# A transformer block on one core: another order for the preparation ahead of its main loop

## The chip, the cores and the metric

The kernel runs on one core of a Trainium2 chip. A core has a matrix engine (TensorE, PE in the profile, with PEld for its weight loads), VectorE (DVE), ScalarE (ACT), GpSimd (POOL) and SyncE (SP), each with an instruction queue of its own, and 16 DMA engines that all queues share. The metric is the device time of one execution in microseconds, as the median of several. The kernel before takes 727.65 us (three runs, 727.61 to 729.59).

## The reference, cut to what matters

One block for 16 samples of 256 tokens and 256 channels, 16 heads of 16 channels. Everything is float32.

```python
c_proj = silu(c) @ W_mod + b_mod          # c: 16 x 256, W_mod: 256 x 1536
shift_a, scale_a, gate_a, shift_m, scale_m, gate_m = split(c_proj, 6)
qkv = (ln(x) * (1 + scale_a) + shift_a) @ W_qkv + b_qkv      # q, k, v
x = x + gate_a * (softmax(q @ k.T * hd**-0.5) @ v @ W_proj + b_proj)
q_c = ln(x) @ W_qc + b_qc;  k_c, v_c = split(ln(context) @ W_kvc + b_kvc)
x = x + softmax(q_c @ k_c.T * hd**-0.5) @ v_c @ W_cproj + b_cproj
x = x + gate_m * (gelu((ln(x)*(1+scale_m)+shift_m) @ W_mlp1 + b_mlp1) @ W_mlp2 + b_mlp2)
```

## The kernel before, in words

Work is cut into 32 units: a self-attention ("s") and a cross-attention ("c") unit for each sample (`seq`, L824). Products that feed the softmax have to be more exact than one pass of the fast matmul type gives. So each operand is split into a high part (rounded to fp32r) and a low part (the rest), and a product is a sum of three: high by high, high by low, low by high (`mm3`, L463, goes through these three for the first half of the 256 input channels, then for the second).

For a unit, its normalised input `xn` is turned by TensorE into channel-major form (`psT`; word `T<n>t`), ScalarE scales it by 1 + scale_a while it rounds (`xTh`, word `T<n>h`), and VectorE makes the rest (`xTl`, word `T<n>l`). The products for keys and queries (`K<n>`, `Q<n>`) give `ps_k` and `ps_q`; ScalarE adds the bias and rounds (`h_k`, `h_q`), VectorE makes the rest (`l_k`, `l_q`), and three DMAs lay these rows into the "stack" `big[n % 3]` (`to_stack`, L523, `send`), in which the score matmuls find high and low parts on neighbouring partitions. A stack must have been zeroed (`z<n>q`, `z<n>k`: on POOL with the suffix p, on ScalarE with a) and have its rows of ones (`one<n>`).

The main loop (L1269) goes in beats, eight for each unit. In the beats of n = -1 only the scores of unit 0 are computed, and their maxima are reduced on VectorE (tile `mx`); the words of the table 'SL' are put between them. From n = 0 on, a beat holds the transposed scores and exponentials of unit n, the scores of unit n + 1, and the projections of later units.

The change touches what stands before that loop. `E_['PRE']` (L55) is a list of words. Each word calls a function that issues instructions on one or several engines (L1110); every engine's instructions, DMA issues on its queue too, keep the order of this list (`InOrder`, L40). So the list is the order of six queues at once, and a waiting instruction holds up all that follows it on its own engine. The words that matter here:

- `load` (L174): x of sample 0 on ScalarE's queue, on SP's queue W_mod for scale, the bias rows, W_qkv for keys, W_mod for shift, W_qkv for queries, x of sample 1, W_qkv for values. The condition `c_sb` is sent before it (L100).
- `silu` and `turn` (L185, L190): silu(c) is c * (tanh(c/2) + 1) / 2. Before: ScalarE's tanh and VectorE's product run on `c_sb`, 16 partitions by 256; then TensorE turns the result (`turn`) into 128 partitions by 32 and ScalarE halves it into `sT`.
- `b<n>` (L165): n matmuls of a tile of zeros into an unused bank; the profile shows each as two instructions.
- `brow`, `bp`, `bro2`: the bias rows, turned into columns.
- `scale`, `sc1`, `shift` (L218 to L224): columns of c_proj from `sT`, eight matmul instructions each, and VectorE's addition of the bias; `bk`, `bq`, `bv` (L227): the shift's share of the biases, from `shift` and the three parts of W_qkv.
- `hik`, `hiq`, `hiv` and `lok`, `loq`, `lov`: the split of W_qkv into `wself`.
- `L<n>a`, `b`, `d`: LayerNorm's statistics (VectorE), the power -1/2 (aggregation on VectorE, power on POOL), the application on VectorE.
- `lg`, `lc`, `lp`, `ld<n>`: loads for the gate, for the cross projection, for the projection, and of x of sample n.
- `K0a`, `K0m`: the key products of unit 0 for output channels 0 to 127 and 128 to 255; `K0h`, `K0l`: `h_k`, `l_k`; `K0x`, `K0w`, `K0yp`: the stack's transfers on SP, SP and POOL.

A DMA issue on SP can also be held by an older one: SP's issue of x of sample 2 stands idle until a part of W_mod has landed.

Of the kernel before, what the change touches and what calls it, by code (L numbers as in the profile page):

```python
# [10 lines left out]
F32 = mybir.dt.float32  # L11
F32R = mybir.dt.float32r
AF = mybir.ActivationFunctionType
ALU = mybir.AluOpType
AX = mybir.AxisListType

P = 128
# [4 lines left out]
def pixart_block(  # L22
# [8 lines left out]
    B, N, H = x.shape  # L31
# [4 lines left out]
    KC = H // P  # L36
# [15 lines left out]
                return tc.keep_in_program_order(i) if self.on else i  # L52
            return issue

    E_ = {'CUT': 8, 'LN': {'s': 'pool', 'c': 'pool', 'q': 'pool'}, 'ON': (1, 1, 1), 'L0': -16, 'L1': 1, 'S0': -7, 'A0': 0, 'T0': 1, 'S1': 5, 'A1': 7, 'L2': 9, 'T1': 9, 'S2': 32, 'AP': 99, 'DV': (0, 1), 'HP': (1, 0), 'BZ': {}, 'AV': {1: [(1, 2), (1, 3)], 9: [(0, 0), (0, 1)]}, 'AHEAD': (0, 0, 0, 0, 0, 2), 'TW': {(21, 6): 'cb', (23, 5): 'u0', (23, 7): 'u1', (25, 2): 'u2', (27, 3): 'u3', (27, 7): 'h2a', (28, 0): 'l2 h0p u5', (28, 2): 'h1p', (28, 4): 'h3p', (28, 7): 'u4 u6', (29, 0): 'l3d', (29, 1): 'l0', (29, 2): 'l1', (29, 7): 'h5p', (30, 1): 'u7 h6d h7p', (30, 3): 'h4p', (31, 1): 'l4 l6d', (31, 2): 'l5d x2', (31, 4): 'l7', (31, 7): 'b2'}, 'BE': 'G0 av P g0 A1 G1 G2 N1 F7 g1 S0 PF s2 p2 G3 a2 aT aL G4 x3 b3 S1 S2 T2 C r0 G5 S3 G6 S4 s3 CF x4 F8 g2 G7 S5 F9 p3 S6 G8 a3 r1 G9 F10 G10 T3 g3 b4 x5 x6 S7 s4 F11 S8 S9 F12 G11 p4 a4 F13 r2 S10 G12', 'XP': 1, 'IL': 1, 'MF': 0, 'SH': 4, 'RAMP': 1, 'HA': 1, 'MP': 16, 'W': (7, 1, 0, 0), 'PRE': 'load L0a z0kp z0qp L0b silu b15 hik turn L0d brow bp z1qa lok T0t lg scale b1 lc sc1 bro2 T0h T0l shift b3 ld2 one0 hiq loq L1a hiv K0a L1b bk K0m L1d bq K0h K0l Q0a L2a T1t T1h lp K0yp K0x z1kp Q0m T1l bv K1a Q0h K0w Q0x Q0yp Q0l lov K1b Q1a Q0w L2b Q1b K1l V0a K1y Q1l z2ka ld3', 'SL': {(-1, 0): 'V0b wm one1 L2c', (-1, 1): 'V1a T2t T2h', (-1, 2): 'K1wp T2p', (-1, 3): 'K1xp L3a Q1yp V1b ga', (-1, 4): 'M0 z2qa Q1xp Q1wp pb L3b vone gs', (-1, 5): 'mods0 ld4', (-1, 6): 'K2a K2m L3p', (-1, 7): 'L3c cb lx gm', (0, 0): 'sp3 mods1', (0, 1): 'sp0', (0, 3): 'sp1', (0, 4): 'sc2', (0, 6): 'one2', (1, 1): 'sp2', (1, 2): 'sp4'}}  # L55

    PE = InOrder(nc.tensor, True)
    ACT, DVE, POOL, SP = (InOrder(e, True) for e in (nc.scalar, nc.vector, nc.gpsimd, nc.sync))

    const = ctx.enter_context(tc.tile_pool(name="const", bufs=1))  # L60
    work = ctx.enter_context(tc.tile_pool(name="work", bufs=2))
# [3 lines left out]
    LONG, SHORT = "gen", "tr"  # L65
    ps_turn = [0]

    def ps_gen(name, tag=None):


        if tag is None and ps_turn[0] is not None:
            ps_turn[0] ^= 1
            tag = (SHORT, LONG)[ps_turn[0]]
        tag = tag or SHORT
        return psum.tile([P, 512], F32, tag=tag, name=name, bufs=2)
# [4 lines left out]
    ident = const.tile([P, P], F32, name="ident")  # L80
# [5 lines left out]
    big = [whole_big[:, 16 * N * i + 16:16 * N * (i + 1) + 16].rearrange("p (a k n) -> p a k n", a=2, k=8)  # L86
           for i in range(3)]
# [8 lines left out]

    BMOD, BQKV, BKVC, BM1 = 0, 12, 20, 24
    BQ, BK, BQC, BKC = 32, 34, 36, 38
    c_sb, th = [work.tile([B, 2, H], F32, tag=t, name=n, bufs=3)[:, 0] for t, n in (("qkh", "c_sb"), ("qkl", "th"))]
    SP.dma_start(c_sb, cond)  # L100
    X = {}

# [7 lines left out]
    brow = const.tile([32, P], F32, name="brow")  # L110
# [26 lines left out]
    sc1 = const.tile([P, 2, 2, B], F32, name="sc1")  # L137
    bT = const.tile([P, 40], F32, name="bT")
    sT = const.tile([P, KC, B], F32, name="sT")
    cb = const.tile([P, H], F32, name="cb")  # L140
# [43 lines left out]

    def f_silu():  # L185
        ACT.activation(dummy, mhalf, AF.Tanh)
        ACT.activation(th, c_sb, AF.Tanh, scale=0.5)
        DVE.scalar_tensor_tensor(th, th, 1.0, c_sb, ALU.add, ALU.mult)

    def f_turn():  # L190
        pst = st[:, 1, 480:]
        for k in range(KC):
            PE.transpose(pst[:, k * B:(k + 1) * B], th[:, k * P:(k + 1) * P], ident[:B, :B])
        ACT.mul(sT.rearrange("p k b -> p (k b)"), pst[:, :KC * B], 0.5)

    odd_rows = []

# [100 lines left out]
    wm = []  # L298
# [9 lines left out]
    gm = []  # L308
# [154 lines left out]
    def mm3(dst, W, f, xT):  # L463

        n = 0
        for k in range(KC):
            for a, b in ((W[0], xT[0]), (W[0], xT[1]), (W[1], xT[0])):
                PE.matmul(dst, a[:, k, f * P:(f + 1) * P], b[:, k],
                          start=(n == 0), stop=(n == 3 * KC - 1))
                n += 1  # L470
# [52 lines left out]
    def to_stack(W, src, bias, dst, which, name):  # L523

        o = Box()
        lo_row = (2, 1)[which]

        o.W, o.src, o.tok, o.name = W, src, False, name  # L530

        def first():
            o.ps = ps_gen(f"ps_{name}", LONG)
            mm3(o.ps[:, 0:N], W, 0, src.xT)

        def third():
            mm3(o.ps[:, N:], W, 1, src.xT)

        def second():
            third()  # L540
            high()

        def high():
            o.hi = work.tile([P, KC, N], F32R, tag="qkh", name=f"h_{name}", bufs=3)
            for f in range(KC):
                ACT.activation(o.hi[:, f], o.ps[:, f * N:(f + 1) * N], AF.Identity, bias=bias[f])

        def low():
            o.lo = work.tile([P, KC, N], F32R, tag="qkl", name=f"l_{name}", bufs=3)
            for f in range(KC):  # L550
                DVE.scalar_tensor_tensor(o.lo[:, f], o.ps[:, f * N:(f + 1) * N], bias[f], o.hi[:, f],
                                         ALU.add, ALU.subtract)

        def low_pool():
            o.lo = work.tile([P, KC, N], F32R, tag="qkl", name=f"l_{name}", bufs=3)
            y = work.tile([P, KC, N], F32, tag="A", name=f"y_{name}", bufs=1)
            for f in range(KC):
                ACT.activation(y[:, f], o.ps[:, f * N:(f + 1) * N], AF.Identity, bias=bias[f])
            POOL.tensor_tensor(o.lo, y, o.hi, ALU.subtract)

        def send(part, q=SP):

            row = (0, 3 - lo_row)[part] if part < 2 else lo_row
            q.dma_start(dst[row:row + 125:4].bitcast(F32), (o.hi if part < 2 else o.lo).bitcast(F32))

        def send_all():
            for part in range(3):
                send(part)

        o.send = send  # L570
        o.parts = [first, second, low]
        o.third = third
        o.low_pool = low_pool
        o.high, o.low = high, low
        o.send_high = lambda: [send(part) for part in range(2)]
        o.send_low = lambda: send(2)
        o.steps = [first, second, lambda: (low(), send_all())]
        return o

# [465 lines left out]
    u0, u1 = units[:2]  # L1045
# [4 lines left out]
    u2 = units[2]  # L1050
# [12 lines left out]
    for n, v in (("0", u0), ("1", u1), ("2", u2)):  # L1063
        word["T" + n + "t"], word["T" + n + "h"], word["T" + n + "l"] = v.T[0].parts
        word["T" + n + "p"] = v.T[0].low_pool
        for c in "KQ":
            o = getattr(v, c)
            word[c + n + "l"] = o.parts[2]
            word[c + n + "m"], word[c + n + "h"] = o.third, o.high
            word[c + n + "p"] = o.low_pool  # L1070
            for q, k in enumerate("xyw"):
                word[f"{c}{n}{k}"] = lambda o=o, q=q: o.send(q)
                word[f"{c}{n}{k}p"] = lambda o=o, q=q: o.send(q, POOL)
# [7 lines left out]
    for n in range(3):  # L1081
        for h, c in enumerate("qk"):
            for e, q in (("", DVE), ("p", POOL)):
                word[f"z{n}{c}{e}"] = lambda n=n, h=h, q=q: q.memset(big[n][:, h].bitcast(F32), 0.0)
            word[f"z{n}{c}a"] = lambda n=n, h=h: ACT.copy(
                big[n][:, h].rearrange("p k (a c) -> p (k a) c", c=P),
                wz.unsqueeze(1).to_broadcast([P, 16, P]))
# [10 lines left out]
    for i in range(5):  # L1098
        word[f"sp{i}"] = lambda i=i: f_split(i)
    word["vone"] = lambda: [POOL.memset(v[:, :, :, HD:], 1.0) for v in vts]  # L1100
    for n, f in (("load", f_load), ("silu", f_silu), ("turn", f_turn), ("brow", f_brow), ("bp", f_bp), ("bro2", f_bro2),
                 ("scale", f_scale), ("sc1", f_sc1), ("shift", f_shift),
                 ("lg", f_loads_g), ("lp", f_loads_p), ("lc", f_loads_c), ("lx", f_loads_x),
                 ("ga", f_ga), ("pb", f_pb), ("gs", f_gs), ("cb", f_cb),
                 ("wm", f_wm), ("mods0", lambda: f_mods(0)), ("mods1", lambda: f_mods(1)), ("sc2", f_sc2), ("gm", f_gm)):
        word[n] = f
# [274 lines left out]
```

## Time and profile before

| what | value |
|---|---|
| median of the runs shown | 727.65 us (727.61 to 729.59) |
| the profiled execution's own time | 728.29 us |
| its span in the trace | 726.5 us, so 1.8 us lie outside it |
| mean granted TensorE clock | 0.997 |
| PE busy | 718.9 us (99%) |
| PEld, ACT, DVE, POOL busy | 633.3, 579.3, 567.8, 526.8 us |
| first score matmul (end of the preparation) | 21.13 us |
| first beat with exponentials | 34.71 us |

PE's busy share counts a matmul as busy from its start to its modelled end, waits for its neighbours too, so 99% does not say that PE is at its peak. All times are microseconds from the span's start.

### The profile page before, as it was taken

How to read it: one execution, taken by the hardware profiler on the slowest of the kernel's cores; microseconds unless marked ns; L12 is line 12 of the kernel's file. 1: busy time of each engine (PE TensorE's matmuls, PEld its weight loads, DVE VectorE, ACT ScalarE, POOL GpSimd, SP SyncE). 2: the span in 40 equal slices, each digit the busy share in tenths (PEclk: the TensorE clock that was granted, in tenths of full speed). 3: DMA queues.
4: the chain of work that ended last, by engine and by line, in shares of the span. 5: the costliest groups of instructions: out<-in, count | busy, mean ns of one | idle time of the engine just before them, and what ended most of it. 6: DMA issues, size and time to landing. Idle time of an engine off the chain costs nothing.

```text
span 726.5 us, 24914 instructions
## 1 busy us (share of the span) xinstructions
PE 718.9 (99%) x10086; PEld 633.3 (87%) x10086; DVE 567.8 (78%) x1208; ACT 579.3 (80%) x1006; POOL 526.8 (73%) x561
## 2 busy tenths in 40 slices
PE   9999999999999999999999999999999999999997
PEld 8788888888888888888888888888878999999997
DVE  4888898989888888888889888888845675676552
ACT  5578898888888888888888888898887677777773
POOL 6766687969687786969687898979746756656643
PEclk9999999999999999999999999999999999999999
DMA  6645333332424343342433444244311414334421
GB/s 208 209 150 176 119 120 143 138 120 105 162 107 161 124 152 124 120 147 112 169 119 137 152 149 161 106 145 142 128 52 54 117 46 117 96 87 111 102 64 39
DMA packets 67110, 90.56 MB, mean 125 GB/s; under 512 B 6194, under 2 KB 38740, under 8 KB 66996
## 3 DMA queue, kind: packets, MB, share of 16 engines
q1 hardware_dynamic: 66164, 86.88, 35.8%
q8 instruction: 80, 1.31, 0.7%
q0 software_dynamic: 560, 1.84, 0.7%
q14 instruction: 34, 0.28, 0.1%
q10 hardware_dynamic: 272, 0.26, 0.1%
HBM read 26.97 MB, written 8.46 MB: 49 GB/s over the span
## 4 chain that ended last, share of the span: by engine, by line
PE 93%; POOL 3%; issue 1%; DVE 1%; ACT 1%; DMA 0%; POOLq 0%; ACTq 0%
PE s L51 18%; PE o L51 16%; PE st L51 15%; PE ph L51 10%; PE ps_P_s L51 4%; PE ps_qc L51 4%; PE ps_v_c L51 4%; PE ps_kc L51 4%; PE ps_q L51 4%; PE ps_v_s L51 3%; PE ps_k L51 3%; PE ps_P_c L51 2%; PE psT_q L51 1%; PE psA_s L51 1%; POOL hl L51 1%
## 5 line engine op out<-in xcount | busy, mean ns | idle before, releaser
L51 DVE TENSOR_REDUCE mx<-s 128x2 f32<-128x512 f32 x504 | 324.7, 683 | 64.3 <-PE s L51 59.0
L51 ACT ACTIVATE pt<-st 128x1024 f32<-128x1024 f32 x252 | 258.9, 1028 | 16.9 <-PE st L51 10.5
L51 PE MATMUL s<-big 63*128 63x256 f32 (+1 forms) x1024 | 185.6, 299 | 0.2
L51 PEld LDWEIGHTS s<-big 63*128 63x128 f32 (+1 forms) x1024 | 133.5, 186 | 19.1 <-DVE l_kc L51 6.6
L51 PE MATMUL st<-big 64*128 64x256 f32 (+1 forms) x1024 | 134.4, 299 | 0.5 <-DMA big<-l_q 0.3
L51 POOL TENSOR_TENSOR hl<-hf,hh 128x512 fp32r<-128x512 f32 x64 | 87.4, 1368 | 63.2 <-ACT hh L51 63.1
L51 PE MATMUL o<-pt,v 128*32 128x256 f32 x2048 | 123.8, 382 | 0.0
L51 PEld LDWEIGHTS st<-big 64*128 64x128 f32 (+1 forms) x1024 | 96.3, 187 | 16.0 <-issue 13.0
L51 PEld LDWEIGHTS o<-pt,v 128*32 128x32 f32 x2048 | 60.0, 109 | 41.4
L51 PE MATMUL ph<-wcross,wself 128*128 128x256 f32 x672 | 85.4, 277 | 0.0
L51 PEld LDWEIGHTS ph<-wcross,wself 128*128 128x128 f32 x672 | 80.4, 188 | 0.0
L51 ACT COPY oT<-o 128x512 f32<-128x512 f32 x63 | 37.0, 587 | 32.7 <-PE o L51 32.7
L51 ACT ACTIVATE hf<-ph,bT 128x256 f32<-128x256 f32 x114 | 47.7, 472 | 18.4 <-PE ph L51 18.4
L51 ACT ACTIVATE hh<-ph,bT 128x256 fp32r<-128x256 f32 x114 | 47.9, 473 | 17.9 <-PE s L51 8.7
L51 PE MATMUL ps_kc<-xTh_c,wcross 64*128 64x256 f32 x256 | 46.6, 291 | 0.0
L51 PE MATMUL s<-big,hh 128*128 128x256 f32 x256 | 45.2, 277 | 0.0
L51 PE MATMUL st<-big,hh 128*128 128x256 f32 x256 | 45.2, 277 | 0.0
L51 PE MATMUL ps_v_c<-wcross,xTh_c 64*128 64x256 f32 x256 | 44.3, 292 | 0.0
L51 PE MATMUL ps_k<-xTh_s,wself 64*128 64x256 f32 (+1 forms) x232 | 43.5, 293 | 0.0
L51 PE MATMUL ps_qc<-xTh_q,wcross 64*128 64x256 f32 x256 | 41.2, 280 | 0.0
L51 PE MATMUL ps_q<-xTh_s,wself 64*128 64x256 f32 (+1 forms) x240 | 40.7, 287 | 0.0
L51 POOL TENSOR_SCALAR xn_c<-c,mv_c,rs_c 128x256 f32<-128x256 f32 x32 | 39.0, 1227 | 1.7
(240 smaller groups left out, 2135.7 us busy)
## 6 DMA issues: line engine op xcount, KB each, us to landing
big<-h_kc SPq DMA_DIRECT2D x32, 256.0 KB
big<-h_qc SPq DMA_DIRECT2D x32, 256.0 KB
big<-h_k SPq DMA_DIRECT2D x30, 256.0 KB
big<-h_q SPq DMA_DIRECT2D x29, 256.0 KB
g<-gd SPq DMA_DIRECT2D x16, 256.0 KB
c<-in_ctx_dram SPq DMA_DIRECT2D x16, 256.0 KB
big<-l_kc SPq DMA_DIRECT2D x16, 256.0 KB
big<-l_qc SPq DMA_DIRECT2D x16, 256.0 KB
```

What stands on the lines that cost most here:

```text
L51: i = f(*a, **k)
```

## The change

The table 'PRE' gets another order, and four words change:

- `silu` now turns `c_sb` itself: two transposes of 16 x 128 on TensorE, then ScalarE's tanh of the turned tile (128 x 32) and its half, and in the new word `th2` VectorE's product, which writes `sT` directly. `turn` is gone.
- The word after it is `b5` and `b3` in place of `b15` (and `b1` in place of `b3` ahead of the key products).
- `scale` and `sc1` now stand ahead of `T0t`.
- `K0a bk K0m` becomes `K0i`, the four high-by-high products, then `shift`, then `K0j`, the other eight, then `bk`.
- `z0qp` (POOL) becomes `z0qa` (ScalarE, behind `hiq`), `z1kp` becomes two halves on POOL: `z1kAp` behind `L0a`, `z1kBp` behind `K0j`.
- `lg` and `lc` move behind `ld2` and `one0`, `lp` follows them; all stand ahead of `K0yp` and `K0x`. `L2a` moves behind `lov`, `Q0h` ahead of `bv`, `L1d` and others by a place or two.

```diff
-... 'PRE': 'load L0a z0kp z0qp L0b silu b15 hik turn L0d brow bp z1qa lok T0t lg scale b1 lc sc1 bro2 T0h T0l shift b3
-  ld2 one0 hiq loq L1a hiv K0a L1b bk K0m L1d bq K0h K0l Q0a L2a T1t T1h lp K0yp K0x z1kp Q0m T1l bv K1a Q0h K0w Q0x
-  Q0yp Q0l lov K1b Q1a Q0w L2b Q1b K1l V0a K1y Q1l z2ka ld3'
+... 'PRE': 'load z0kp b5 silu L0a th2 z1kAp L0b z1qa b3 brow bp L0d scale sc1 b1 T0t hik lok T0h bro2 b1 K0i T0l shift
+  K0j z1kBp hiq loq ld2 lg one0 lc lp z0qa L1a L1b bk L1d K0h hiv K0l Q0a bq K0yp K0x T1t T1h K0w Q0m T1l Q0h bv K1a
+  Q0x Q0yp Q0l Q0w lov L2a K1b Q1a L2b Q1b K1l V0a K1y Q1l z2ka ld3'
...
     def f_silu():
         ACT.activation(dummy, mhalf, AF.Tanh)
-        ACT.activation(th, c_sb, AF.Tanh, scale=0.5)
-        DVE.scalar_tensor_tensor(th, th, 1.0, c_sb, ALU.add, ALU.mult)
-
-    def f_turn():
         pst = st[:, 1, 480:]
         for k in range(KC):
-            PE.transpose(pst[:, k * B:(k + 1) * B], th[:, k * P:(k + 1) * P], ident[:B, :B])
-        ACT.mul(sT.rearrange("p k b -> p (k b)"), pst[:, :KC * B], 0.5)
+            PE.transpose(pst[:, k * B:(k + 1) * B], c_sb[:, k * P:(k + 1) * P], ident[:B, :B])
+        ACT.activation(th[:, :KC * B], pst[:, :KC * B], AF.Tanh, scale=0.5)
+        ACT.mul(th[:, KC * B:2 * KC * B], pst[:, :KC * B], 0.5)
+
+    def f_th2():
+        DVE.scalar_tensor_tensor(sT.rearrange("p k b -> p (k b)"), th[:, :KC * B], 1.0, th[:, KC * B:2 * KC * B],
+                                 ALU.add, ALU.mult)
...
+        def some(products):
+            for n, (a, k, f) in enumerate(products):
+                PE.matmul(o.ps[:, f * N:(f + 1) * N], W[a // 2][:, k, f * P:(f + 1) * P], src.xT[a % 2][:, k],
+                          start=(a == n == 0), stop=(a == 2 and k == KC - 1), skip_group_check=True)
+
+        def high_high():
+            o.ps = ps_gen(f"ps_{name}", LONG)
+            some([(0, k, f) for k in range(KC) for f in range(2)])
+
+        def rest():
+            some([(a, k, f) for a in (1, 2) for k in range(KC) for f in range(2)])
...
+            word[c + n + "i"], word[c + n + "j"] = o.by_part
...
+            for i, part in enumerate("AB"):
+                word[f"z{n}{c}{part}p"] = lambda n=n, h=h, i=i: POOL.memset(
+                    big[n][:, h, 4 * i:4 * i + 4].bitcast(F32), 0.0)
```

More of the change, by code (lines that the diff above doesn't have):

```diff
@@ L53, in __getattr__ @@
             return issue
-    E_ = {'CUT': 8, 'LN': {'s': 'pool', 'c': 'pool', 'q': 'pool'}, 'ON': (1, 1, 1), 'L0': -16, 'L1': 1, 'S0': -7, 'A0': 0, 'T0': 1, 'S1': 5, 'A1': 7, 'L2': 9, 'T1': 9, 'S2': 32, 'AP': 99, 'DV': (0, 1), 'HP': (1, 0), 'BZ': {}, 'AV': {1: [(1, 2), (1, 3)], 9: [(0, 0), (0, 1)]}, 'AHEAD': (0, 0, 0, 0, 0, 2), 'TW': {(21, 6): 'cb', (23, 5): 'u0', (23, 7): 'u1', (25, 2): 'u2', (27, 3): 'u3', (27, 7): 'h2a', (28, 0): 'l2 h0p u5', (28, 2): 'h1p', (28, 4): 'h3p', (28, 7): 'u4 u6', (29, 0): 'l3d', (29, 1): 'l0', (29, 2): 'l1', (29, 7): 'h5p', (30, 1): 'u7 h6d h7p', (30, 3): 'h4p', (31, 1): 'l4 l6d', (31, 2): 'l5d x2', (31, 4): 'l7', (31, 7): 'b2'}, 'BE': 'G0 av P g0 A1 G1 G2 N1 F7 g1 S0 PF s2 p2 G3 a2 aT aL G4 x3 b3 S1 S2 T2 C r0 G5 S3 G6 S4 s3 CF x4 F8 g2 G7 S5 F9 p3 S6 G8 a3 r1 G9 F10 G10 T3 g3 b4 x5 x6 S7 s4 F11 S8 S9 F12 G11 p4 a4 F13 r2 S10 G12', 'XP': 1, 'IL': 1, 'MF': 0, 'SH': 4, 'RAMP': 1, 'HA': 1, 'MP': 16, 'W': (7, 1, 0, 0), 'PRE': 'load L0a z0kp z0qp L0b silu b15 hik turn L0d brow bp z1qa lok T0t lg scale b1 lc sc1 bro2 T0h T0l shift b3 ld2 one0 hiq loq L1a hiv K0a L1b bk K0m L1d bq K0h K0l Q0a L2a T1t T1h lp K0yp K0x z1kp Q0m T1l bv K1a Q0h K0w Q0x Q0yp Q0l lov K1b Q1a Q0w L2b Q1b K1l V0a K1y Q1l z2ka ld3', 'SL': {(-1, 0): 'V0b wm one1 L2c', (-1, 1): 'V1a T2t T2h', (-1, 2): 'K1wp T2p', (-1, 3): 'K1xp L3a Q1yp V1b ga', (-1, 4): 'M0 z2qa Q1xp Q1wp pb L3b vone gs', (-1, 5): 'mods0 ld4', (-1, 6): 'K2a K2m L3p', (-1, 7): 'L3c cb lx gm', (0, 0): 'sp3 mods1', (0, 1): 'sp0', (0, 3): 'sp1', (0, 4): 'sc2', (0, 6): 'one2', (1, 1): 'sp2', (1, 2): 'sp4'}}
@@ new lines, in pixart_block @@
+    E_ = {'CUT': 8, 'LN': {'s': 'pool', 'c': 'pool', 'q': 'pool'}, 'ON': (1, 1, 1), 'L0': -16, 'L1': 1, 'S0': -7, 'A0': 0, 'T0': 1, 'S1': 5, 'A1': 7, 'L2': 9, 'T1': 9, 'S2': 32, 'AP': 99, 'DV': (0, 1), 'HP': (1, 0), 'BZ': {}, 'AV': {1: [(1, 2), (1, 3)], 9: [(0, 0), (0, 1)]}, 'AHEAD': (0, 0, 0, 0, 0, 2), 'TW': {(21, 6): 'cb', (23, 5): 'u0', (23, 7): 'u1', (25, 2): 'u2', (27, 3): 'u3', (27, 7): 'h2a', (28, 0): 'l2 h0p u5', (28, 2): 'h1p', (28, 4): 'h3p', (28, 7): 'u4 u6', (29, 0): 'l3d', (29, 1): 'l0', (29, 2): 'l1', (29, 7): 'h5p', (30, 1): 'u7 h6d h7p', (30, 3): 'h4p', (31, 1): 'l4 l6d', (31, 2): 'l5d x2', (31, 4): 'l7', (31, 7): 'b2'}, 'BE': 'G0 av P g0 A1 G1 G2 N1 F7 g1 S0 PF s2 p2 G3 a2 aT aL G4 x3 b3 S1 S2 T2 C r0 G5 S3 G6 S4 s3 CF x4 F8 g2 G7 S5 F9 p3 S6 G8 a3 r1 G9 F10 G10 T3 g3 b4 x5 x6 S7 s4 F11 S8 S9 F12 G11 p4 a4 F13 r2 S10 G12', 'XP': 1, 'IL': 1, 'MF': 0, 'SH': 4, 'RAMP': 1, 'HA': 1, 'MP': 16, 'W': (7, 1, 0, 0), 'PRE': 'load z0kp b5 silu L0a th2 z1kAp L0b z1qa b3 brow bp L0d scale sc1 b1 T0t hik lok T0h bro2 b1 K0i T0l shift K0j z1kBp hiq loq ld2 lg one0 lc lp z0qa L1a L1b bk L1d K0h hiv K0l Q0a bq K0yp K0x T1t T1h K0w Q0m T1l Q0h bv K1a Q0x Q0yp Q0l Q0w lov L2a K1b Q1a L2b Q1b K1l V0a K1y Q1l z2ka ld3', 'SL': {(-1, 0): 'V0b wm one1 L2c', (-1, 1): 'V1a T2t T2h', (-1, 2): 'K1wp T2p', (-1, 3): 'K1xp L3a Q1yp V1b ga', (-1, 4): 'M0 z2qa Q1xp Q1wp pb L3b vone gs', (-1, 5): 'mods0 ld4', (-1, 6): 'K2a K2m L3p', (-1, 7): 'L3c cb lx gm', (0, 0): 'sp3 mods1', (0, 1): 'sp0', (0, 3): 'sp1', (0, 4): 'sc2', (0, 6): 'one2', (1, 1): 'sp2', (1, 2): 'sp4'}}
@@ L98, in pixart_block @@
     BQ, BK, BQC, BKC = 32, 34, 36, 38
-    c_sb, th = [work.tile([B, 2, H], F32, tag=t, name=n, bufs=3)[:, 0] for t, n in (("qkh", "c_sb"), ("qkl", "th"))]
+    c_sb, th = [work.tile([p, 2, H], F32, tag=t, name=n, bufs=3)[:, 0]
+                for p, t, n in ((B, "qkh", "c_sb"), (P, "qkl", "th"))]
     SP.dma_start(c_sb, cond)
@@ L534, in first @@
             mm3(o.ps[:, 0:N], W, 0, src.xT)
+        def some(products):
[7 more added lines that the diff above has]
+            some([(a, k, f) for a in (1, 2) for k in range(KC) for f in range(2)])
+        o.by_part = high_high, rest
         def third():
@@ L1100, in pixart_block @@
     word["vone"] = lambda: [POOL.memset(v[:, :, :, HD:], 1.0) for v in vts]
-    for n, f in (("load", f_load), ("silu", f_silu), ("turn", f_turn), ("brow", f_brow), ("bp", f_bp), ("bro2", f_bro2),
+    for n, f in (("load", f_load), ("silu", f_silu), ("th2", f_th2), ("brow", f_brow), ("bp", f_bp), ("bro2", f_bro2),
                  ("scale", f_scale), ("sc1", f_sc1), ("shift", f_shift),
```

## The prediction

> **What bounds the kernel now.** I read the page first: PE is the bound of the whole, and its last-ending chain runs on PE nearly throughout.
>
> ```profile
> span 726.5 us, 24914 instructions
> PE 718.9 (99%) x10086; PEld 633.3 (87%) x10086; DVE 567.8 (78%) x1208; ACT 579.3 (80%) x1006; POOL 526.8 (73%) x561
> ...
> PE 93%; POOL 3%; issue 1%; DVE 1%; ACT 1%; DMA 0%; POOLq 0%; ACTq 0%
> ```
>
> The change leaves the loop as it is. So the question is when the loop's first score matmul starts, and whether all behind it comes earlier by the same amount. Second view: the chain of waits, its first 31 us (start, duration, work).
>
> ```profile
> 1.85 3.49 POOL big L51 x2
> 5.42 0.24 POOL rs_s L51
> ...
> 6.96 0.87 PE psT_s L51 x4
> 7.83 0.80 PE st L51 x8
> ...
> 9.18 0.99 PE st L51 x8
> 10.18 0.76 PE s L51 x6
> 10.94 0.95 PE ps_k L51 x6
> 11.88 0.84 PE st L51 x8
> 12.73 0.80 PE ps_k L51 x6
> 13.53 0.84 PE st L51 x8
> 14.37 0.81 PE ps_q L51 x6
> 15.18 0.45 PE psT_s L51 x4
> ...
> 18.30 2.69 DMA big<-l_q
> ```
>
> POOL zeroes unit 0's stack (two memsets) before it can do the power for LayerNorm; so `xn` and its turn (`psT_s`, ending at 7.83) are late. Then PE does scale (7.83), shift (9.18), fillers, half the keys, `bk`, the other half, `bq`, and so on; at 18.30 `l_q` is sent. Third view: the timeline, for the steps beside PE.
>
> ```profile
> 1.04 5.44 PE L51 MATMUL s<-wz 128*128 128x128 f32 x30 [1.04 <-DVE wz L51]
> 3.18 0.41 ACT L51 ACTIVATE th<-c_sb 16x256 f32<-16x256 f32 x1 [0.47 <-DMA c_sb<-in_cond_dram]
> 4.48 0.30 DVE L51 BATCH_NORM_AGGREGATE mv_s<-st_s 128x2 f32<-128x6 f32 x2
> 6.29 0.66 ACT L51 CAST wself<-wf 128x512 fp32r<-128x512 f32 x1 [2.70 <-DMA wf<-in_L_xcond_W_qkv_dram]
> 6.41 0.29 PE L51 MATMUL st<-ident,th 16*128 16x16 f32 x2
> 6.86 0.18 ACT L51 ACTIVATE sT<-st 128x32 f32<-128x32 f32 x1
> 7.03 1.35 POOL L51 TENSOR_TENSOR wself<-wf,wself 128x512 fp32r<-128x512 f32 x1 [0.58 <-ACT wself L51]
> 7.01 0.42 ACT L51 COPY bp<-brow 32x256 f32<-32x256 f32 x1
> 7.34 1.89 ACT L51 CAST big<-wz 128x2048 fp32r<-128x2048 f32 x1
> 8.73 0.19 DVE L51 TENSOR_TENSOR cpT<-st,bT 128x32 f32<-128x32 f32 x1 [1.51 <-PE st L51]
> 9.58 0.84 ACT L51 ACTIVATE xTh_s<-psT_s,sc 128x256 fp32r<-128x256 f32 x2
> 10.45 0.88 DVE L51 SCALAR_TENSOR_TENSOR xTl_s<-psT_s,sc,xTh_s 128x256 fp32r<-128x256 f32 x2 [1.08 <-ACT xTh_s L51]
> 15.30 0.74 DVE L51 BATCH_NORM_STATS2 st_s<-x 128x6 f32<-128x256 f32 x2
> 20.25 2.44 POOL L51 TENSOR_SCALAR xn_s<-x,mv_s,rs_s 128x256 f32<-128x256 f32 x2
> 21.13 0.50 PE L51 MATMUL st<-big 63*128 63x256 f32 x4 [0.34 <-DMA big<-l_q]
> 23.71 0.60 PE L51 MATMUL psT_s<-ident,xn_s 128*128 128x128 f32 x4
> ```
>
> The first score matmul, at 21.13, waits for `l_q`, 0.34 us after PE had nothing else to do. `xTh` waits until 9.58 for the scale columns and for the bias columns ahead of it on ACT, 1.75 us after its turn is done.
>
> **The change part by part.**
>
> *The condition.* It lands by 3.18. Five fillers instead of fifteen are ten instructions instead of 30: at the row's mean of 0.18 us (5.44 / 30) they end near 2.9, at twice the 0.13 of the later six (0.76 / 6) at 3.6. The two transposes (0.29), tanh and half (0.18 each, from the row of `sT`, which has the new size) follow by about 4.3; `th2`, priced at the 0.19 of an addition of that size, waits for LayerNorm's statistics on VectorE, which end at 4.48. So `sT` is there at about 4.7 instead of 7.04. The old tanh (0.41) and its product go; the turn itself stays. Scale's eight matmuls (0.80) then end by 6.2 if its weights have come. Their landing has no row; they were sent before the key weights, which are there at 6.29, so the bounds are 4.7 and 6.3, and scale ends between 5.7 and 7.1. Its columns are wanted only when `psT` is done (7.46, next step), after 0.19 for the bias and about as much for `sc1`. The added cost is therefore nothing up to the late end, and 0.1 us there.
>
> *LayerNorm of unit 0.* One memset of 1.75 (half of 3.49) and half of another (0.87) end at about 4.5 (1.85 + 2.62). The aggregation, moved behind `th2`, ends at 4.97 (4.78 + 0.19); that is now the later one, so POOL starts at about 5.05 instead of 5.42, and `psT` ends at 7.46 instead of 7.83: 0.37 gained. ScalarE now zeroes another stack first (`z1qa`, 1.89, about 4.3 to 6.2), then the bias rows (`bp` 0.42 and a short copy), then `hik` (0.66), which ends at about 7.3. That still leaves `xTh` free to start at 7.49. So `xTh` gains 9.58 - 7.49 = 2.09 us.
>
> *Keys.* Now PE has between `xTh` and `bk`: four high products, shift, eight products; before, shift lay ahead of `xTh`. Six products take 0.80, so 0.133 each. If the first two need only the first piece of `xTh` (half of 0.84): 7.49 + 0.42 + 0.03 = 7.94, two products to 8.21; the second piece is done at 8.33, two more to 8.63; shift (0.99) to 9.62; `K0j` (8 x 0.133 = 1.07) to 10.69; `bk` (0.84) to 11.53. If they wait for both pieces, everything from there is 0.26 later: 11.79. The other inputs of `K0j` are ready: `xTl` 0.88 after `xTh`, 9.3; the low key weights (1.35 behind `hik`), 8.7. The zeroing of `z0q` on ScalarE (1.89 behind `hiq`, about 9.2 to 11.1) lies ahead of `h_k`, wanted at about 11.8; it has 0.6 us to spare, and without it `h_k` is late by what is over.
>
> *From there to the scores.* The order on PE is the old one without `K0m`: `Q0a` 0.81, `bq` 0.84, turn 0.45, so unit 1's turn ends at 13.63 (or 13.89) instead of 15.63: 2.00 (or 1.74) gained. Behind it the steps are the old ones (`xTh` of unit 1, `h_q`, `l_q`, 2.69 of DMA), so the score matmul moves by the same. PE must also be done with the products for unit 1 and the first values, a stretch which ended at 20.8 (21.13 - 0.34) and contains the same work, so it moves by as much. 0.1 to 0.3 us of handovers that my packed sum leaves out lower this to 1.45 to 2.0; I take **1.75**, and 19.4 for the first scores.
>
> *Loads.* In both versions SP's loads all stand ahead of the stacks' transfers:
>
> ```profile
> 4.68 0.47 SPq L51 DMA_DIRECT2D wga<-in_L_xcond_W_mod_dram  x1
> 7.49 0.38 SPq L51 DMA_DIRECT2D x<-in_x_dram  x1
> 9.80 0.44 SPq L51 DMA_DIRECT2D wp_f<-in_L_xcond_W_proj_dram  x1
> 14.43 0.66 SPq L51 DMA_DIRECT2D big<-h_k  x1
> 12.00:14.40 2.40, 2.40 (x22) 2.40 (x22) 1.23 (x6) 0.83 (x2) 1.30 (x3) 1.00 0.04 12
> 21.13:34.71 13.58, 13.14 (x91) 8.84 (x91) 12.20 (x22) 7.19 (x11) 10.58 (x16) 1.00 0.67 213
> ```
>
> (the last two: stretch, its length, busy time of PE, PEld, DVE, ACT, POOL, granted clock, DMA share, GB/s). The DMA engines are nearly empty (0.04) from 12.00 to the first stack transfer, which now comes at about 12.7. The same bytes are sent in another order, so that reordering is worth nothing here; if all four loads slipped by 0.7 us, a transfer of `h_k` would meet their end, and `l_q` four microseconds later would not.
>
> *Behind the first score.* From 21.13 to 34.71 VectorE is busy for 12.20 of 13.58 us, PE for 13.14: the stretch has no slack of its own that would swallow an earlier start, and everything that it needs moves with it. One thing moves less: `L2a` (0.74) now comes after `lov` on VectorE, so POOL's `xn` of unit 2 starts about 0.8 earlier, ends at 21.9, and its turn on PE would like to start at 22.0. It has 0.1 to spare instead of 1.0.
>
> The sum against the profiled execution's own time: 728.29 - 1.75 = 726.54. The median of the runs shown is 0.64 below that execution, so 727.65 - 1.75 = **725.9**; the likeliest case's own range is 725.2 to 726.6.
>
> **The rivals.**
>
> *A cold start, on the slow side.* The granted clock (stretch, length, PE busy, clock, DMA) falls to half once, here its first and last slices:
>
> ```profile
> 39.00:40.00 1.00, 1.00 (x16) 0.51 0.99 372
> 42.00:43.00 1.00, 1.00 (x18) 0.78 0.00 0
> ```
>
> That is about 3.4 us at half speed, 39.0 to 42.4 (by the mean of the last slice). At the start the 30 fillers average 0.18 us, while six of the same kind later take 0.76, or 0.13 each: PE starts slow there too, and 20 of the instructions that keep it busy are taken away. If the clock rises one such stretch later, to about 8.3, scale takes 0.8 more and the turn 0.45 more, of which some 0.8 reaches the end: 726.7, still not slower than before. If it stays low, or falls again, until about 11.7, then products, shift, rest and `bk` (0.53 + 0.99 + 1.07 + 0.84 = 3.43) also take twice as long: 3.43 + 0.8 - 1.75 = 2.5 slower, **730.1**. It decides from the point where the slow clock lasts beyond about 9.6. Against it: PE still has work from 1.04 on without a long gap, and between 5 and 8.3 the old version is as thin and keeps its clock.
>
> The Trainium skill, "TensorE: Matmul & The Clock Gate" (Part 1), speaks against taking fillers out: it says that the array runs at half clock until a window of some 3.4 us of sustained activity has passed, and that these windows run free of the kernel's start. The 3.4 us of half clock above agree with its window; no run here yet shows a start with fewer fillers. By that rule alone the time would depend on where the windows fall, between 725.9 and the rival's figure.
>
> *The dip goes.* With the program moved by 1.75 us the half-clock stretch at 39 to 42.4 may not occur. Its work would fit in half, so 1.7 more: **724.2**. For it: the clock looks at stretches of time, and the work moves under them. Against: a thin piece of work can be caught as well 1.75 us earlier.
>
> *A new wait.* `xn` of unit 2 is late for its turn (0.1 to spare), or `z0q` for `h_k`, or the key weights for `hik`: 0.5 to 1.7 of the gain is lost, **726.9** and up to 727.6. For it: three margins of 0.1 to 0.6. Against: VectorE binds the beats at 22 too, which covers some of it. That the change does nothing at all would need a start fixed by something later than all this; the chain shows none.
>
> **How the numbers follow.** Forecast 0.58, cold start 0.08, dip gone 0.17, new wait 0.17. A measurement of this kernel tells about 0.3% (2.2 us, 725.5) from no change. Faster by more than that: the dip's case and a quarter of the forecast's, 0.31; slower: the cold start and a little for the unforeseen, 0.10; the rest, 0.59, within. The range goes down to the dip's 724.2 and up to 727.9, where the lost gain ends; the cold start is outside.
>
> **What would show it.** In the profile after: `sT` by 4.8, `xTh` at 7.5, `h_k` at 11.8 to 12.0, `l_q` sent at 16.3 to 16.8, first scores at 19.1 to 19.7, the next stretch of the loop at about 33.0 in place of 34.71. It is wrong if the first scores move by 1.75 and the span does not, if fillers after 5 us still take 0.2 each, or if a turn of `xn` ends more than 0.3 after its place.

## The result, and the profile after

The changed kernel is slower. Its median is 734.47 us against 727.98 of the kernel before, 21 executions of each; the ratio is 1.0055 with a 95% interval of 1.0035 to 1.0075. This ratio, like those further down, weighs all executions and lies near that of the means (1.0052); the two medians alone give 1.0089. The forecast was 725.9.

The median does not tell all: the executions fall in two groups. Of the changed kernel's 21, fifteen take 734.05 to 735.10 us and six take 725.58 to 729.40. Of the 21 of the kernel before, nineteen take 727.39 to 729.59 and two take 735.58 and 735.67. So both kernels can take some 7 us longer; with the change this is the usual case, and the profiled execution (734.63) is one of it.

The page's head, and its list of cores with the mean granted clock:

```profile
span 732.8 us, 24876 instructions
PE 725.7 (99%) x10068; PEld 639.6 (87%) x10068; DVE 573.4 (78%) x1208; ACT 580.8 (79%) x1007; POOL 523.6 (71%) x561
...
core 0: 732.8 us, clock 1.000
```

By that clock nothing is wrong. The chain of waits of the changed kernel (start, duration, work) says otherwise:

```profile
1.04 2.50 PE s L51 x10
3.55 0.32 PE st L51 x2
3.87 1.82 PE s L51 x7
5.69 1.83 PE st L51 x8
7.52 0.03 issue
...
7.84 1.68 DVE sc L51
...
9.62 0.48 ACT xTh_s L51
...
10.14 1.22 PE ps_k L51 x4
11.37 1.52 PE st L51 x8
12.89 1.89 PE ps_k L51 x8
14.78 1.52 PE st L51 x8
16.30 1.47 PE ps_q L51 x6
...
28.65 0.43 PE st L51 x4
```

Eight products for the bias columns (`st`, x8) take 1.52 us here and 0.84 before; six query products (`ps_q`) 1.47 and 0.81. Everything on PE takes nearly twice as long. Two other things are to be seen. The scale columns (`st` at 5.69) start within the forecast's 4.7 to 6.3, but they take 1.83 and end at 7.52, later than its 7.1, and 1 + scale (`sc`) takes 1.68 us on VectorE. And `xTh` starts at 9.62, no earlier than the 9.58 of before.

How long PE is slow is read from its weight loads, which have one size through this stretch (stretch, length, PEld busy with the count of loads, granted clock, DMA share, GB/s); first the changed kernel, then the kernel before:

```profile
12.00:14.00 2.00, 2.00 (x11) 1.00 0.01 4
24.00:26.00 2.00, 2.00 (x11) 1.00 0.84 323
28.00:30.00 2.00, 1.60 (x16) 1.00 0.94 290
```

```profile
12.00:14.00 2.00, 2.00 (x19) 1.00 0.02 7
```

Eleven loads fit into 2 us, where before it were 19. This lasts until about 27.3, where a single load goes from 0.33 to 0.19 us; the third row is the first score matmul:

```profile
26.85 0.33 PEld L51 LDWEIGHTS ps_q<-xTl_s,wself 128*128 128x128 f32 x1
27.42 0.19 PEld L51 LDWEIGHTS ps_q<-xTl_s,wself 128*128 128x128 f32 x1
28.58 0.50 PE L51 MATMUL st<-big 63*128 63x256 f32 x4
```

The clock column reads 1.00 all the while: it shows a clock that falls during the run, as at 39 us before, but not one that never rose.

The first score matmul starts at 28.58 instead of 21.13, 7.45 us later. Of these, 0.04 are at `xTh` (9.62 - 9.58), and 7.41 lie between `xTh` and the scores (18.96 against 11.55). The span grew by 6.3. Most of the other 1.1 came back where the profiled execution of before has its half-clock stretch (39.0 to 42.4), which this one has not: an `xn` on POOL ahead of that place is 7.6 late (40.39 against 32.78), the first product with `v` (`o`) behind it 6.6 (50.5 against 43.9).

### The profile page after: what moved, and what is told of

Same layout as the page of the kernel before. It is cut to its first block, busy times and chain, and to the rows that moved or that the text cites. A ratio compares the mean times of both kernels' runs of the same rounds, so it can differ in the third digit from the quotient of the medians.

```text
span 732.8 us, 24876 instructions
## 1 busy us (share of the span) xinstructions
PE 725.7 (99%) x10068; PEld 639.6 (87%) x10068; DVE 573.4 (78%) x1208; ACT 580.8 (79%) x1007; POOL 523.6 (71%) x561
## 4 chain that ended last, share of the span: by engine, by line
PE 94%; POOL 2%; DVE 1%; issue 1%; ACT 1%; POOLq 0%; ACTq 0%; DVEq 0%
PE s L51 18%; PE o L51 16%; PE st L51 16%; PE ph L51 10%; PE ps_q L51 4%; PE ps_qc L51 4%; PE ps_P_s L51 4%; PE ps_kc L51 4%; PE ps_k L51 3%; PE ps_v_c L51 3%; PE ps_v_s L51 2%; PE ps_P_c L51 2%; PE psT_q L51 1%; PE ps_h L51 1%; PE psA_s L51 1%
## 5 line engine op out<-in xcount | busy, mean ns | idle before, releaser
L51 POOL TENSOR_TENSOR hl<-hf,hh 128x512 fp32r<-128x512 f32 x64 | 85.8, 1343 | 64.5 <-ACT hh L51 64.4
L51 PE MATMUL ps_k<-xTh_s,wself 64*128 64x256 f32 (+1 forms) x232 | 45.0, 303 | 0.1
```

The source lines that it names most:

```text
L51: i = f(*a, **k)
```

## The experiments

Two theories stood at the start. *Clock*: PE starts slow and is made fast by a long stretch of continuous work; ahead of the condition's turn the change left 10 of 30 instructions on the zero tile (the "fillers", `b<n>`), and 6 stand between that turn and the scale columns (`b5` stands ahead of `silu`, `b3` behind it). *Order*: the new order of products, or the slow addition, is what costs.

**Fillers taken from the kernel before.**

```diff
-L0b silu b15 hik turn
+L0b silu b5 hik turn
```

> The kernel before with one edit: b15 is b5, so 10 instructions on the zero tile ahead of the turn of the condition in place of 30; no order of products, no zeroing and no load is touched. Theory (clock): PE's slow start lasts until it has been kept busy for a whole stretch of some 3.4 us; with the fillers ending near 3.6 that does not come until the dense key and query products of unit 1, so most executions take 733 to 736 us, as most of the changed kernel's do, and weight loads of 128 x 128 take 0.33 us instead of 0.19 until about 25 us. Rival (order): the slow executions of the changed kernel come from its order of products and adds, then this takes 727 to 728.5 like the kernel before.

Measured: 734.58 us, all six executions between 732.7 and 736.5; ratio to the kernel before 1.0083 (1.0065 to 1.0101). This one edit makes the kernel before as slow as the changed one. Its weight loads come slowly first, at full pace later:

```profile
12.00:14.00 2.00, 2.00 (x11) 1.00 0.00 0
18.00:20.00 2.00, 2.00 (x19) 1.00 0.30 110
```

The clock theory holds for what starts it: fewer fillers are enough. The rise came at about 16 us in this profile, sooner than the expectation's 25.

**Fillers given back to the changed kernel**, as many as before, behind the turn of the condition.

```diff
-L0b z1qa b3 brow bp
+L0b z1qa b10 brow bp
```

> The changed kernel with its second group of fillers b3 made b10, so that 30 instructions on the zero tile stand ahead of the scale columns, as in the kernel before. Theory (clock): the clock rises near 5 us as before; scale moves to about 6.7 and most executions take 725 to 727 us. Rival (order): still 733 to 736 us in most executions.

Measured: 736.05 us, ratio 1.0107 (1.0090 to 1.0123), five of five above 735. By the letter the rival won. The profile shows something else: the clock was raised, and fell again. PE's busy time by stretch, and the timeline of that place:

```profile
6.00:8.00 2.00, 2.00 (x18) 1.00 1.03 330
8.00:10.00 2.00, 1.41 (x11) 1.00 1.08 353
10.00:12.00 2.00, 0.98 (x7) 0.94 0.90 269
12.00:14.00 2.00, 2.00 (x10) 0.50 0.01 4
28.00:30.00 2.00, 2.00 (x15) 0.79 0.74 224
```

```profile
8.17 1.29 POOL L51 TENSOR_TENSOR wself<-wf,wself 128x512 fp32r<-128x512 f32 x1 [2.42 <-ACT wself L51]
8.33 2.06 DVE L51 TENSOR_SCALAR sc<-cpT 128x32 f32<-128x32 f32 x1
9.41 0.95 POOL L51 MEMSET big<- 128x1024 f32 x1
10.49 0.84 ACT L51 ACTIVATE xTh_s<-psT_s,sc 128x256 fp32r<-128x256 f32 x2 [2.40 <-DVE bT L51]
11.02 0.75 PE L51 MATMUL ps_k<-xTh_s,wself 128*128 128x256 f32 x3 [1.61 <-ACT xTh_s L51]
```

Here the granted clock does show it: 0.50 from about 11.8 to 28.8. It also says what the slow pace of the changed kernel is, since the weight loads at a recorded 0.50 are as long as there, eleven in 2 us:

```profile
12.00:14.00 2.00, 2.00 (x11) 0.50 0.01 4
```

PE had stood 1.61 us for `xTh`, and `xTh` for the addition `sc`, which ended at 10.39 with POOL's second instruction (10.36). So a second cause was at hand, VectorE's addition held up by POOL, and the next run takes it away.

**1 + scale from PSUM**, with the ten fillers.

```diff
     def f_scale():
-        cols(cpT[:, 2:4], [wm1], sT, bT[:, BMOD + 2:BMOD + 4], "scale")
+        pst = st[:, len(spots) % 2, 2 * B * len(spots):]
+        bias = bT[:, BMOD + 2:BMOD + 4]
+        cols(cpT[:, 2:4], [wm1], sT, bias, "scale")
+        DVE.scalar_tensor_tensor(sc1[:, 0], pst[:, :2 * B].rearrange("p (n b) -> p n b", b=B), 1.0,
+                                 bias.unsqueeze(2).to_broadcast([P, 2, B]), ALU.add, ALU.add)
     def f_sc1():
-        DVE.tensor_scalar(sc1[:, 0], cpT[:, 2:4], 1.0, None, ALU.add)
+        pass
```

> The same with ten fillers, and 1 + scale is made by VectorE from the PSUM bank of the scale products in place of from the copy in SBUF. In the changed kernel this 128 x 32 addition took 1.68 us instead of 0.18 and ended with POOL's work beside it. Theory (shared port): an operation of VectorE that only reads and writes SBUF waits for POOL's running instructions, one that reads PSUM does not; it then takes about 0.2 us, xTh starts up to 1 us earlier than with the ten fillers alone, and the median is 0.3 to 1 us lower. Rival: the 1.68 us is a wait for the result of the addition before it, and nothing changes.

Measured: 727.56 us, eleven of eleven executions between 726.48 and 728.64; ratio to the kernel before 0.9989 (0.9980 to 0.9997). The addition runs beside POOL's subtraction and is done in 0.18:

```profile
8.66 1.29 POOL L51 TENSOR_TENSOR wself<-wf,wself 128x512 fp32r<-128x512 f32 x1 [2.81 <-ACT wself L51]
8.70 0.18 DVE L51 SCALAR_TENSOR_TENSOR sc<-st,bT 128x32 f32<-128x32 f32 x1
9.28 0.84 ACT L51 ACTIVATE xTh_s<-psT_s,sc 128x256 fp32r<-128x256 f32 x2 [0.70 <-PE psT_s L51]
```

Its median is 8.5 us under the version with the stalled addition, where 0.3 to 1 was expected. Of that, 1.2 us is `xTh` itself (10.49 to 9.28); the rest goes with the clock, which stays up (19 weight loads from 12 to 14 us in place of 11).

**The same addition without the fillers**, to see whether the stall alone was to blame.

```diff
     (b5 and b3 as in the changed kernel)
-        DVE.tensor_scalar(sc1[:, 0], cpT[:, 2:4], 1.0, None, ALU.add)
+        DVE.scalar_tensor_tensor(sc1[:, 0], ...)          # from PSUM, as above
```

> The changed kernel with its own few fillers, and 1 + scale made from PSUM. Theory (shared port and clock): the addition takes 0.2 us, xTh starts when the turn of xn is done, 9.0 instead of 9.62, and the slow clock stays, so most executions stay at 733 to 735 us, some 0.5 us less than the changed kernel's. Rival: the stalled addition is what makes PE idle and keeps its clock low; then most executions fall to 725 to 727 us.

Measured: 734.72 us, ratio 1.0063 (1.0040 to 1.0086), three of twelve executions at 728.1 to 729.2, eight at 734.4 to 735.4 and one at 739.25, which the ratio leaves out. `xTh` starts at 9.0, as expected, and the clock stays low. So the stall cost the changed kernel 0.6 us of `xTh` and is not the cause of its times near 734; the fillers are. The median is not lower than the changed kernel's, which the expectation had wrong.

**POOL's second instruction moved away**, the addition left in SBUF, with the ten fillers.

```diff
-shift K0j z1kBp hiq loq
+shift K0j hiq loq
-bq K0yp K0x T1t
+bq K0yp K0x z1kBp T1t
```

> The changed kernel with ten fillers as before (its median was 736.05), 1 + scale made in SBUF as in the changed kernel, but the second half of the zeroing of unit 1's key rows moved on POOL from behind K0j to behind K0x, so that only the low key weights' subtraction runs on POOL beside the addition. Theory (shared port): the addition now ends with that subtraction, at about 9.4 to 9.7 instead of 10.36, and takes 1 to 1.4 us instead of 2.06; if PE's shorter wait no longer lowers its clock, the median is 727.5 to 728.5, else 735. Rival (wait for the addition before it): it still takes 2 us.

Measured: 733.60 us, ratio 1.0042 (1.0018 to 1.0065); four of twelve at 728.6 to 729.3, eight at 733.5 to 734.1 with a mean clock of 0.991.

```profile
9.44 1.30 POOL L51 TENSOR_TENSOR wself<-wf,wself 128x512 fp32r<-128x512 f32 x1 [3.71 <-ACT wself L51]
9.60 1.17 DVE L51 TENSOR_SCALAR sc<-cpT 128x32 f32<-128x32 f32 x1
```

The addition now ends (10.77) with POOL's one instruction (10.74). Its length follows POOL's work, 1.17 against 2.06, and not the addition ahead of it, so the rival falls. The end comes later than the expected 9.4 to 9.7, since POOL's split itself starts 1.3 us later in this execution (9.44 against 8.17). PE's wait for `xTh` is 0.72 us in place of 1.61, and the clock stays up in four of twelve executions in place of none of five; these counts are too small to show that the shorter wait is why.

The Trainium skill states a rule that fits ("SBUF — State Buffer", "SBUF: two separate sides"): VectorE, in its two-port modes, and GpSimd hold a shared pair of ports exclusively for a whole instruction, and the other one blocks. The rows agree, 2.06 and 1.17 us for an addition of 0.18, though none shows in which mode the addition ran. They add that VectorE did not get in between two POOL instructions that follow each other closely.

**Fewer fillers**, with the addition from PSUM: 12 and 10 in all, cut by the turn of the bias rows.

```diff
-z1qa b3 brow bp L0d scale sc1 b1 T0t
+z1qa b3 brow b4 bp L0d scale sc1 T0t
```

> With 1 + scale from PSUM; the second group of ten fillers is cut into b3, the turn of the bias rows, b4 (12 in all with the first five), and the filler between scale and the turn of xn is gone. Theory: the clock still rises near 5 us; bias columns are there at 5.9 instead of 7.7, scale ends by 7.3, xTh starts at about 8.0 to 8.3 instead of 9.28, and the median is 726.0 to 726.8 against 727.56 with ten fillers. Rival: with fewer fillers the clock stays low in half of the executions or more, 733 to 735.

```diff
-z1qa b3 brow bp L0d scale sc1 b1 T0t
+z1qa b3 brow b2 bp L0d scale sc1 T0t
```

> As the version with b3, bias rows, b4, but b2 in place of b4 (10 fillers in all instead of 12). Theory (a whole stretch of 3.4 us must be busy): the clock rises early in fewer executions than with 12 and 15, so the times fall in two groups, near 726 and near 733 to 735. Rival (only the stalled addition mattered): all near 726.

Measured: with 12 fillers 727.05 us (ratio 1.0011, 0.9972 to 1.0049), seven of twelve executions at 726.2 to 727.2, the others at 733 to 736; with 10 fillers 734.91 us (1.0053, 1.0024 to 1.0082), four of twelve at 726.4 to 729.3. With the 8 of the run above it were three of twelve, with 15 eleven of eleven. So the share of executions below 730 us goes with the amount of filler work. The counts are small, and what the clock did is known only from the mean clock of each execution and from the one profile of each version; both profiles here are of executions near 735 us (734.58 and 735.23), so the expected `xTh` of 8.0 to 8.3 was not seen. These two versions also lack the filler between scale and the turn of `xn`, which was not tried alone.

**The old order of the key products**, in the version with ten fillers behind the turn and the addition from PSUM.

```diff
-T0h bro2 b1 K0i T0l shift K0j z1kBp hiq
+T0h bro2 b1 T0l shift K0a z1kBp hiq
-L1b bk L1d
+L1b bk K0m L1d
```

> The fast version of before (ten fillers, 1 + scale from PSUM, 727.56) with the old order on PE: shift straight after the turn of xn, then half of the keys, bk, the other half, in place of high-by-high products, shift, the rest, bk. Theory that the prediction used (the new order brings the keys forward): the median is 0.3 to 0.7 us higher. Rival: shift fills PE while xTh is made, so the old order is as fast or up to 0.6 us faster, and the gain lies in the earlier xTh alone.

Measured: 727.41 us, ratio 0.9980 (0.9957 to 1.0003); ten of twelve at 726.8 to 728.0, two at 731.3 and 731.5 with a mean clock of 0.993. Against 727.56 that is no loss, and the rival holds. From `xTh` to the first score matmul there are 11.5 us with the old order (9.81 to 21.29) and 11.7 with the new (9.28 to 20.97); the chains, old order first:

```profile
21.29 0.50 PE st L51 x4
```

```profile
20.97 0.50 PE st L51 x4
```

High-by-high products first bring nothing.

**All fillers in one row ahead of the turn of the condition**, the addition from PSUM; 13 and 15.

```diff
-load z0kp b5 silu L0a th2 z1kAp L0b z1qa b3 brow bp L0d scale sc1 b1 T0t hik
+load z0kp b13 z1qa silu L0a z1kAp L0b L0d th2 brow bp T0t scale sc1 hik
```

> 1 + scale from PSUM; all fillers in one row ahead of the turn of the condition (b13, no hole between them, 26 instructions), the zeroing of unit 1's query rows ahead of the tanh on ScalarE, LayerNorm's application ahead of the condition's product on VectorE, the turn of xn ahead of scale. Theory (a whole stretch without a hole raises the clock): the row from 1.04 to about 5.6 raises it in most executions, more often than 12 fillers with a hole did (7 of 12), xTh starts at about 8.2, and the fast executions take 726.0 to 727.0. Rival: the number of fillers decides, not the hole; then about half of the executions stay at 733 to 736.

> The same with b15, as many as in the kernel before. Theory: the clock rises in nearly all executions, xTh starts 0.3 to 0.5 us later than with b13, and the fast executions take 726.3 to 727.4, so the median lies 0.8 to 1.5 us under the kernel before. Rival: PE's wait between scale and the keys lowers the clock again, 733 to 734 with a granted clock of 0.991.

Measured: 13 fillers 734.25 us (1.0057, 1.0028 to 1.0086), three of twelve at 726.2 to 726.6, the rest with a mean clock of 0.988 to 0.991; 15 fillers 729.96 us (1.0025, 0.9999 to 1.0052), six of twelve at 726.7 to 727.9. Those clocks say that it was raised in these too and lost again, here with 13:

```profile
8.00:9.20 1.20, 1.20 (x10) 1.00 1.06 357
9.20:10.00 0.80, 0.43 (x3) 0.85 1.07 339
10.00:12.00 2.00, 2.00 (x12) 0.50 0.91 264
```

PE stands 0.37 us (0.80 - 0.43) for `xTh`, after the 16-column products of scale, and 0.1 us after that wait the clock falls. The wait alone is not shown to be the cause: in the profile with 15 fillers it has the same length and ends at 9.26, and the clock falls at 11.4, with PE busy all the time between. What comes just before a fall in both is a thin stretch, scale's products and the wait, in the second also the 16-column products of shift. The kernel before has three fillers at this place, the changed one a single one.

**Those three given back.**

```diff
-T0h bro2 b1 K0i
+T0h bro2 b3 K0i
```

> The version with fifteen fillers in front, with the one filler ahead of the key products made three again, as many as the kernel before has there. Theory (thin work between scale and the keys lowers the clock that the first fillers raised): the executions at 732 and 735 with a clock of 0.988 to 0.991 (6 of 12) become rare, at most 3 of 12, and the median is 727.0 to 728.0; the fast executions lose at most 0.3 us, since PE waits there for xTh anyway. Rival: the clock that falls has to do with the stretch before scale, and half of the executions stay slow.

Measured: 727.19 us, ten of ten executions at 726.5 to 728.4; ratio to the kernel before (728.29 on that chip) 0.9975, interval 0.9957 to 0.9993. Six of twelve lost the clock with one filler at the keys, none of ten with three. That is no guarantee: the kernel before has three there too, and 3 of its 22 executions beside this version (6 of 35 in an earlier group) show a mean clock of 0.990 to 0.993 and take 732 to 734.5. This version is faster than both kernels, than the kernel before by 0.25%, which rests on ten executions. `xTh` starts at 8.97, and the scores at 20.65, 0.48 earlier than before:

```profile
8.97 0.84 ACT L51 ACTIVATE xTh_s<-psT_s,sc 128x256 fp32r<-128x256 f32 x2 [0.92 <-DVE bT L51]
20.65 0.50 PE L51 MATMUL st<-big 63*128 63x256 f32 x4 [0.42 <-DMA big<-l_q]
```

**The other place for the fillers, with the same three at the keys.**

```diff
-z1qa b10 brow bp L0d scale sc1 b1 T0t ... T0h bro2 b1 K0i
+z1qa b3 brow b7 bp L0d scale sc1 T0t ... T0h bro2 b3 K0i
```

> Ten fillers behind the turn of the condition and 1 + scale from PSUM (727.56, 11 of 11 fast), with the bias rows' turn after the first three of the ten, no filler between scale and the turn of xn, and three at the keys. Theory: the clock stays up in nearly all executions, xTh starts 0.2 to 0.4 us earlier than 9.28, and the median is 727.0 to 727.5, 0.6 to 1 us under the kernel before. Rival: the bias rows' turn among the fillers makes a hole that keeps the clock low in some executions, as with twelve fillers.

Measured: 727.87 us, ratio 0.9993 (0.9981 to 1.0004), all twelve between 726.2 and 730.3. No execution lies near 734, but in the profile the fillers run slowly for longer and `xTh` starts at 9.57, later than the expectation's 8.9 to 9.1; the median missed its 727.0 to 727.5.

## Why the prediction was wrong, step by step

**The step that failed first is the fillers.** The prediction counted them only as time that the condition waits for, gave the twenty instructions fewer no price in the sum, and put everything behind them at the old full-speed durations ("scale's eight matmuls (0.80)", `bk` 0.84). Measured in the profiled execution: scale 1.83, `bk` 1.52, and so on until 27.3 us. Behind `xTh` the way to the first score took 18.96 us in place of 11.55; the same order with the clock up took 11.69 (9.28 to 20.97), so 7.27 of the 7.45 us at the first score go with the slow clock. The run with nothing but fewer fillers in the kernel before shows that they are enough.

**The cold-start rival had the mechanism, and its price and chance were too low.** It gave the slow side 730.1 and 0.08. The price let the clock rise at 11.7 at the latest, for no reason that a row gave; it rose at 27.3 in the profiled execution. The argument against it was "PE still has work from 1.04 on without a long gap, and between 5 and 8.3 the old version is as thin and keeps its clock". The first half is no reason: from 10.14 to 27.3 us PE has no gap in the trace at all and is slow until the end of it. The second half misreads the prediction's own row: the old fillers run from 1.04 to 6.48 (1.04 + 5.44), so up to there the old version is not thin.

The Trainium skill ("TensorE: Matmul & The Clock Gate", Part 1) says that a window of some 3.4 us of sustained activity raises the clock. Here PE was busy by the trace for 17 us before it rose, so "busy" as the trace shows it isn't what counts. Four groups of 16-column products (`st`, 1.52 each) break up that time; the longest stretch without one, the key and query products from 23.02 on, is the one in which the clock rose, 4.3 us after its start. That fits the theory that thin products don't count, but what exactly counts no run here shows.

**The second step that failed is 1 + scale**, "about as much" as the 0.19 of the addition before it. It took 1.68 us in the profiled execution, since the change put it at 7.84, beside POOL's split of the key weights (7.29 to 8.59) and the half of the zeroing that was moved there (8.53 to 9.48). Before, it ran at 8.96 in 0.18, when POOL was idle. With the clock raised the stall also costs the clock: 736.05 against 727.56. The prediction listed what each moved word waits for by data and never what would run beside it on POOL.

**The steps that held.** The condition was at `sT` at 4.55 (forecast: by 4.8), and POOL started the power at 4.80 (5.05). The reordered loads changed nothing that a row shows: DMA share 0.01 from 12 to 14 us, as the prediction had it. From `xTh` to the scores, new order against old, the prediction's own sum was a small loss (from 7.49 to 19.4, 11.9 against 11.55); measured 11.7 against 11.5. Its whole gain was the 2.09 us at `xTh`, and that did not come in any profiled execution: 9.62 in the changed kernel, 8.97 in the best version, 8.73 at the earliest (15 fillers in front). One slip lies in the working of the scale columns: 4.7 + 0.80 is 5.5, where it has 6.2 in one place and 5.7 in the other; the sum does not use it. In two executions of the changed kernel the time is 725.58 and 726.09, near the forecast's 725.9, with a mean clock of 0.999 and 1.000 (the other four of the fast group have 0.994 to 0.997); they have no profile, so whether they ran as the prediction said is open.

**The dip rival** priced the loss of the half-clock stretch at 39 us at 1.7. Of 23 executions of the kernel before on one chip, thirteen with a mean clock of 0.999 or more take 727.27 to 728.05, and nine with 0.996 to 0.998, as the profiled one of before has, take 728.38 to 729.69 (one more has 0.992 and takes 731.26). That is 1.1 us between the two medians (727.63 and 728.77), and it comes and goes without any change; which part of the program ran slowly in them no profile shows. **The new-wait rival** (unit 2's `xn` late, 0.1 us to spare) can be read in the best version: `xn` ends at 22.98 and its turn starts at 23.24, with nothing lost there.

Open are the rule by which the clock rises and falls, and why one execution raises it and the next does not; the runs give shares of executions, not the rule.

## What to carry to other kernels

Work that has no result can still have a price when it is taken away: before counting filler matmuls as free, ask what raised TensorE's clock and what keeps it up, and look for it in the durations of equal instructions, since the granted-clock column shows no clock that never rose. In this kernel, which starts with few and thin products, the clock came up and stayed up most often where dense work stood both at the start and in the place where PE waits. And when a small VectorE operation from SBUF to SBUF is moved, look at what POOL runs at that moment; reading PSUM instead took the stall away.

## What the runs showed of the hardware that was not expected

- PE ran for 26 us with hardly a gap at the pace of a half clock (11 weight loads in 2 us instead of 19, as in a stretch with a recorded clock of 0.50), while the granted clock was reported as 1.00.
- The share of executions below 730 us goes with the filler work ahead of the scale columns: 5 fillers none of 6 (in the old order), 8 fillers 6 of 21 and 3 of 12, 10 fillers 4 of 12, 12 fillers 7 of 12, 15 fillers 11 of 11 and 10 of 12 (from the second 8 on with the fillers in two groups and the addition from PSUM). With all of them in one row it is 13 fillers 3 of 12 and 15 fillers 6 of 12, where the mean clocks say that it rose and fell again.
- A raised clock fell 0.1 us (13 fillers in front) and 2.2 us (15) after a wait of PE of 0.37 us behind products of 16 columns; with three fillers (six instructions) in that place it was kept in ten of ten executions, and in the kernel before, which has them too, in 19 of 22 beside them.
- A VectorE addition of 128 x 32 took 0.18 us alone and 1.17, 1.68 and 2.06 us beside POOL instructions, ending each time within 0.04 us of POOL's.
